# Second layer's routed experts computed on tokens sorted by expert, in 54 blocks of 128 laid among the attention's half steps, with the routing of all batches at once

## The chip, the cores and the metric

One core of one Trainium2 chip runs the whole program. The core has a matrix engine (TensorE; PE in the profile, its weight loads PEld), a vector engine (VectorE, DVE), an engine for functions and copies (ScalarE, ACT), a general engine (GpSimd, POOL) and an engine that here only issues transfers (SyncE, SP). Each engine works through its own program in order; engines wait for one another by semaphores, and data between DRAM and the on-chip memories moves by DMA, issued from a queue on one of the engines. Matrix products land in PSUM, a small memory of eight banks of 2 KB per partition; the rest of the on-chip data is in SBUF, 128 partitions wide.

The metric is the time of one execution in microseconds (us) on the device. All times below are in us unless marked ns.

## The reference, cut to what matters

The input is 2048 tokens (4 batches of 512) of 256 numbers, all in float32. There are two layers, each adding an attention and a mixture of experts, both of the normalised input, to the stream:

```python
xn = layernorm(x)
x = x + attention_0(xn) + experts_0(xn)   # 1 head of 256; 16 experts of width 176, 4 per token, and a shared one of width 352
xn = layernorm(x)
x = x + attention_1(xn) + experts_1(xn)

# attention_1: 8 groups of 4 query heads, head size 8, 512 keys per batch
sim = einsum('bgrsd,bgtd->bgrst', q, k) / sqrt(8)
out = softmax(sim) @ v                     # then a 256x256 projection

# experts_1: 7 routed experts and a shared one, all 256 -> 256 -> 256
def ffn(x, w1, wg, w2): return silu(x @ w1) * (x @ wg) @ w2
output = ffn(x, Ws1, Wsg, Ws2)
p = softmax(x @ gate_w + gate_b)
_, top = top_k(p + biases, 3)
w = p[top] / sum(p[top])                   # a weight for each of the 3 chosen experts
for e in range(7):
    output += ffn(x, W1[e], Wg[e], W2[e]) * (weight of e for this token, 0 if not chosen)
```

The softmax of the second attention has 32 heads x 512 x 512 scores per batch, with a contraction of only 8 numbers.

## The kernel before

**Layer 0.** After the attention of layer 0 the tokens are routed for all batches (`route`), sorted by expert into 79 slots of 128 rows, and each slot runs through `turn`, `gate_up`, `turn_back` and `down` (L576 to L640): rows are gathered from DRAM by an indirect DMA on POOL (L578), turned by TensorE (L586), multiplied by the weights of the slot's expert, which a register picks, and the result is copied (L637) and written to a DRAM table `y_rows` by a DMA on SP (L638). Later `combined` gathers each token's four rows from that table (L959, on POOL) and adds them with their shares on DVE (L978).

**Before the main loop** (L1076 to L1123). Batch 0 of layer 0 is combined, normalised and turned, its queries and keys are made (`project`), its experts are chosen (`choose`), and the pieces of the first layer's shared expert for all batches (`shared_pieces`) are laid between. The maxima of the first two units of attention are taken here (L1105).

**The main loop** (L1137 to L1197). The second attention runs in 32 units, (batch, unit) with 8 units of 4 heads in a batch. A unit is 4 tiles of 128 keys, each done in two *half steps*. A half step issues, in program order:

- a chore (`chore`, see below);
- `score_max` (L740): two matmuls of 32x512 for the unit two ahead, into the two banks `pa`, of which there is one copy;
- `score` (L779): two matmuls for the unit at hand, into `pb` (two copies);
- `take_max` (L752): one DVE reduction of 128x1024 out of `pa`;
- `exponentials` (L794): two ScalarE instructions of 128x512 out of `pb`;
- on every second half step `values` (L802) of the tile before, four matmuls; after a unit's last tile also `context`: a ScalarE copy (L816) and eight DMAs on SP (L820, L826);
- one *piece* of the experts.

`shift` closes a unit: a DVE transpose and 16 small DMAs on SP (L765) that put the maxima into the queries. The last two units have no unit two ahead; they run as 8 double steps (L1167 to L1183) with two pieces each.

**The experts before** are dense: every token runs through all 7 routed experts and the shared one. `expert_pieces` (L897) yields for each batch and each of the 8 experts four times a pair of pieces: `hidden` (L863, two matmuls of 128x512) with `gated` on each second one (a ScalarE tanh L875 and two DVE instructions L876, L877), and `down` (L882, two matmuls of 128x256, and a DVE instruction L893 that multiplies by the token's weight and adds to the stream). So pieces of `hidden` and of `down` alternate, one to a half step: 256 pieces, in 256 half steps.

**Chores** (L1038), one per half step: for batch b+1, while batch b's attention runs, they do layer 0's `combined`, the moments, `normalised`, `project` with its 28 DMAs on SP, and `choose`, which finds the three experts of a token and their weights; then `project_out` of batch b-1. `quotients` (L828) inverts the sums of the exponentials and sends them through DRAM.

**What sets the order.** TensorE, DVE and ScalarE run in the order written by hand. The order of the DMAs on SP and of the work on POOL is made by a scheduler. A tile has a fixed number of copies (`bufs`); who writes a copy again waits for the last reader of its former content, a DMA's end included. In PSUM before: `pa` two banks, `pb` two, `po`, `ph`, `pg` and `py` one each.

Of the kernel before, what the change touches and what calls it, by code (L numbers as in the profile page):

```python
# [40 lines left out]
W1P = 12  # L41
# [4 lines left out]
def two_layer_kernel(  # L46
# [67 lines left out]
    def normalised(layer: int, b: int, pool, psum, bo, tag: str, bufs: int, store=None, room=None):  # L114


        mv = stats[layer][:, ts(b, NQ), :]
        rstd = pool.tile([P, NQ], F32, tag="rstd", name=f"rstd{layer}_{b}")
        nc.vector.tensor_scalar(rstd, mv[:, :, 1], EPS, None, ALU.add)
        nc.scalar.activation(rstd, rstd, AF.Sqrt)  # L120
        nc.vector.reciprocal(rstd, rstd)
        yield
        for t in range(NQ):
            xn = (room or pool.tile)([P, H], F32, tag="xg" if room else "xn", name=f"xn{layer}_{b}_{t}")
            nc.vector.tensor_scalar(
                xn, xs[b][:, t, :], mv[:, t, 0:1], rstd[:, t : t + 1], ALU.subtract, ALU.mult
            )
            if store is not None:
                nc.gpsimd.dma_start(out=store[ts(b * NQ + t, P), :], in_=xn)
            yield "PE"  # L130
            pt = psum.tile([P, HC, P], F32, tag=tag, name=f"ptn{layer}_{b}_{t}", bufs=bufs)
            for c in range(HC):
                nc.tensor.transpose(pt[:, c, :], xn[:, ts(c, P)], ident)
            nc.scalar.copy(xnT[b][:, :, ts(t, P)], pt)
            if t == NQ - 1:
                nc.gpsimd.tensor_tensor(
                    xs[b], xs[b], bo.unsqueeze(1).to_broadcast([P, NQ, H]), ALU.add
                )
            yield
# [16 lines left out]
    y_rows = dram.tile([NS0 * P, H], F32, tag="y_rows", name="y_rows")  # L156

# [3 lines left out]
    with tc.tile_pool(name="w0", bufs=1, side="right") as w0:  # L161
# [17 lines left out]
        wqkv1s = whole(const, wqkv1, "wqkv1s")  # L179
        wo1s = whole(const, wo1, "wo1s")  # L180
        gate1s = whole(const, gate1, "gate1s")
# [12 lines left out]
        with tc.tile_pool(name="rt", bufs=1) as rt, tc.tile_pool(name="a0", bufs=2) as a0, tc.tile_pool(  # L194
            name="a0p", bufs=2, space=PSUM
        ) as a0p, tc.manual_schedule(engines={ENG.PE, ENG.DVE, ENG.Activation}):
            def counting(n: int, step: int, at: int, name: str):

                t = rt.tile([P, n], F32, tag=name, name=name)
                nc.gpsimd.iota(  # L200
                    t,
                    pattern=[[step, n]],
                    base=at,
                    channel_multiplier=1 if name == "tok" else 0,
                    allow_small_or_imprecise_dtypes=True,
                )
                return t

# [5 lines left out]
            def room(shape, dtype, tag: str, name: str):  # L214
                return w0.tile(shape, dtype, tag=tag, name=name, bufs=8)

            moments(0, 0, a0)
            first = normalised(0, 0, a0, a0p, bo, "pt", 2, xn_rows, room)
            next(first), next(first)
# [29 lines left out]
            for b in range(B):  # L249
                if b > 0:  # L250
                    first = normalised(0, b, a0, a0p, bo, "pt", 2, xn_rows, room)
                for _ in first:
                    pass
                if b + 1 < B:
                    moments(0, b + 1, a0)
                values0(b)

            lane = counting(P, 1, 0, "lane")
            slot = counting(NS0, 1, 0, "slot")
            tok = counting(NT, P, 0, "tok")  # L260
            full = counting(NT, P, 0, "full")
            ones = rt.tile([P, P], F32, tag="ones", name="ones")
            nc.gpsimd.memset(ones, 1.0)
            before = rt.tile([P, P], F32, tag="before", name="before")
            nc.gpsimd.affine_select(
                out=before,
                in_=ones,
                compare_op=ALU.is_gt,
                fill=0.0,
                base=0,  # L270
                pattern=[[1, P]],
                channel_multiplier=-1,
            )

            def summed(src, n: int, inner: int, name: str):

                bufs = []
                for i in range(2):
                    t = rt.tile([P, (8 + n) * inner], F32, tag=f"sum{i}", name=f"{name}{i}")
                    nc.gpsimd.memset(t[:, 0 : 8 * inner], 0.0)  # L280
                    bufs.append(t)
                nc.vector.tensor_copy(bufs[0][:, 8 * inner :], src)
                for i, d in enumerate((1, 2, 4, 8)):
                    x, y = bufs[i % 2], bufs[1 - i % 2]
                    nc.vector.tensor_tensor(
                        y[:, 8 * inner :],
                        x[:, 8 * inner :],
                        x[:, (8 - d) * inner : (8 - d + n) * inner],
                        ALU.add,
                    )  # L290
                return bufs[0][:, 8 * inner :]

            def route():
# [9 lines left out]
                top = rt.tile([P, NT, 8], F32, tag="top", name="top0")  # L303
                for t in range(NT):
                    nc.vector.max(out=top[:, t, :], in_=pr[:, t, :])
                    if t % 8 == 7:
                        yield
                nc.vector.memset(top[:, :, K0:8], -1.0)
                rest = rt.tile([P, NT, WP], F32, tag="rest", name="rest0")
                for t in range(NT):  # L310
                    nc.vector.match_replace(
                        out=rest[:, t, :],
                        in_to_replace=top[:, t, :],
                        in_values=pr[:, t, :],
                        imm_value=-2.0,
                    )
                    if t % 8 == 7:
                        yield

                mask = rt.tile([P, NT, E0], F32, tag="mask", name="mask0")  # L320
                nc.vector.tensor_tensor(mask, pr[:, :, 0:E0], rest[:, :, 0:E0], ALU.not_equal)
# [7 lines left out]
                upto = summed(cnt[:, 0, :], NT, E0, "ut")  # L329
                yield  # L330
                total = rt.tile([P, E0], F32, tag="total", name="total")
                nc.vector.tensor_copy(total, upto[:, (NT - 1) * E0 : NT * E0])
                pos = rt.tile([P, NT, E0], F32, tag="pos", name="pos")
                pflat = pos.rearrange("p t e -> p (t e)")
                nc.vector.tensor_tensor(pflat, upto, cnt[:, 0, :], ALU.subtract)
                nc.vector.tensor_tensor(pflat, pflat, cnt[:, 1, :], ALU.add)

                yield

                more = rt.tile([P, E0, NT], F32, tag="more", name="more")  # L340
                nc.vector.tensor_tensor(
                    more,
                    total.unsqueeze(2).to_broadcast([P, E0, NT]),
                    full.unsqueeze(1).to_broadcast([P, E0, NT]),
                    ALU.is_gt,
                )
                need = rt.tile([P, E0], F32, tag="need", name="need")
                nc.vector.reduce_sum(out=need, in_=more, axis=AX.X)
                yield
                end = summed(need, E0, 1, "en")  # L350
                base = rt.tile([P, E0], F32, tag="base", name="base")
                nc.vector.tensor_tensor(base, end, need, ALU.subtract)
                nc.vector.tensor_scalar(base, base, float(P), None, ALU.mult)

                yield

                of = rt.tile([P, NS0], F32, tag="of", name="of")
                half = (NS0 + 1) // 2
                for at in (0, half):
                    n = min(half, NS0 - at)  # L360
                    past = rt.tile([P, half, E0], F32, tag="past", name=f"past{at}")
                    nc.vector.tensor_tensor(
                        past[:, 0:n, :],
                        slot[:, at : at + n].unsqueeze(2).to_broadcast([P, n, E0]),
                        end.unsqueeze(1).to_broadcast([P, n, E0]),
                        ALU.is_ge,
                    )
                    nc.vector.reduce_sum(out=of[:, at : at + n], in_=past[:, 0:n, :], axis=AX.X)
                    yield
                nc.vector.tensor_scalar(off, of, float(E0 - 1), float(W0P), ALU.min, ALU.mult)  # L370

                yield
                nc.vector.tensor_tensor(
# [10 lines left out]
                for t in ith:  # L384
                    nc.gpsimd.memset(t[:, :, 0:8], 0.0)
# [274 lines left out]
    with tc.tile_pool(  # L660
# [236 lines left out]
        def expert_pieces():  # L897
# [16 lines left out]
            for t in range(NQ):  # L914
                down(*last[:2], t, last[2])
# [366 lines left out]
```

## Time and profile before

| what | us |
|---|---|
| median of 9 executions | 1330.07 (1325.77 to 1334.39) |
| the profiled execution | 1333.38 |
| its span (first to last instruction) | 1331.4 |
| mean granted TensorE clock in it | 0.973 of full speed |
| layer 0: attention | 0 to 165 |
| layer 0: the 79 slots | 165 to 360 |
| before the main loop | 360 to 474.8 |
| main loop, half steps 0 to 28 | 474.8 to 565.2 |
| main loop, half steps 29 to 190 | 565.2 to 1114.8 |
| main loop, half steps 191 to 239 | 1114.8 to 1272.7 |
| 8 double steps and the end | 1272.7 to 1331.4 |

The stage borders are starts of instructions of `score_max` or of the last units' scores. The main loop is cut at half steps 29 and 191, where the changed program changes what it lays between.

How to read the profile: one execution is recorded by the hardware. A page gives the busy time of each engine, the busy share and the granted TensorE clock (in tenths of full speed) in 40 equal slices, the chain of work that ended last with the share of each engine and line, and groups of instructions of the same line: form, count, busy time and mean duration, and how long the engine was idle just before them and on whose account. A timeline lists instructions by start, a window sums the busy time of each engine in a stretch. SPq is a queue of DMA issues on SP. Matmuls are pipelined, so their durations overlap; differences of starts are the safer measure.

### The profile page before, as it was taken

The numbers are of one execution on the slowest core, as the hardware profiler recorded it, in microseconds if no ns is written. First come the engines' busy times: TensorE is split into PE (matmuls) and PEld (weight loads), VectorE is DVE, ScalarE is ACT, GpSimd is POOL, SyncE is SP. The second block draws the span as 40 slices with busy tenths as digits, with TensorE's granted clock in tenths as the row PEclk, the third lists the DMA queues.
The fourth block names the chain that finished last, engine by engine and source line by source line (L and its number), as shares of the span: only waits on it lengthen the run. The fifth ranks groups of instructions, "written<-read, shape, count | busy, mean of one in ns | idle before, by whom it ended". The sixth has DMA issues, their size and how long they took to land.

```text
span 1331.4 us, 17659 instructions
## 1 busy us (share of the span) xinstructions
PE 1264.3 (95%) x6068; PEld 598.4 (45%) x6068; DVE 723.0 (54%) x1390; ACT 460.9 (35%) x929; POOL 189.2 (14%) x205
## 2 busy tenths in 40 slices
PE   5889999999999899999999999998999999999995
PEld 4456677777655333333323334432333433333332
DVE  5476244444452676546656656566654655465531
ACT  3321322222212025443434443342543334344342
POOL 4100263333050130000012000013000000000000
PEclk9899999999999689999999999998999999999998
DMA  9300133333133010001011001011000100000000
GB/s 359 128 1 8 56 117 108 107 104 107 62 125 147 15 48 4 10 10 25 16 29 39 8 5 30 13 33 55 4 10 9 26 24 5 9 23 4 10 8 24
DMA packets 43159, 64.04 MB, mean 48 GB/s; under 512 B 18816, under 2 KB 33120, under 8 KB 42176
## 3 DMA queue, kind: packets, MB, share of 16 engines
q1 hardware_dynamic: 33808, 34.00, 8.7%
q0 software_dynamic: 8064, 22.42, 5.8%
q10 hardware_dynamic: 1200, 6.51, 1.3%
q8 instruction: 49, 0.80, 0.2%
q14 instruction: 38, 0.31, 0.1%
HBM read 42.31 MB, written 14.81 MB: 43 GB/s over the span
## 4 chain that ended last, share of the span: by engine, by line
PE 89%; DVE 4%; DMA 2%; SPq 1%; issue 1%; ACT 1%; POOL 1%; ACTq 0%; DVEq 0%; POOLq 0%
PE pa L740 18%; PE ph L863 18%; PE py L882 10%; PE po L802 9%; PE pg L604 7%; PE py L628 5%; PE ps L927 3%; PE po L502 2%; PE pqk L463 2%; PE sc L471 2%; PE pa L620 1%; PE px L586 1%; PE po L844 1%; PE pys L941 1%; PE pv L240 1%
## 5 line engine op out<-in xcount | busy, mean ns | idle before, releaser
L794 ACT ACTIVATE ex<-pb 128x512 f32<-128x512 f32 x496 | 269.3, 595 | 452.3 <-PE pb L779 452.3
L752 DVE TENSOR_REDUCE mx<-pa 128x2 f32<-128x1024 f32 x248 | 302.8, 1221 | 154.7 <-PE pb L779 146.1
L740 PE MATMUL pa<-k,q 32*128 32x512 f32 x960 | 272.2, 643 | 14.4 <-DVE mx L752 14.4
L779 PE MATMUL pb<-q,k 32*128 32x512 f32 x960 | 272.7, 643 | 0.0
L882 PE MATMUL py<-ew,a 128*128 128x256 f32 x512 | 146.6, 409 | 1.7 <-DVE x L893 1.7
L882 PEld LDWEIGHTS py<-ew,a 128*128 128x128 f32 x512 | 87.7, 191 | 115.9 <-issue 105.2
L802 PE MATMUL po<-ex,v 128*32 128x512 f32 x1024 | 137.9, 610 | 0.0
L740 PEld LDWEIGHTS pa<-k,q 32*128 32x128 f32 x960 | 72.2, 184 | 144.2 <-DVE mx L752 78.3
L863 PE MATMUL ph<-xnT,ewg 128*128 128x512 f32 x256 | 131.3, 637 | 0.0
L863 PE MATMUL ph<-xnT,ew 128*128 128x512 f32 x256 | 130.3, 632 | 0.0
L893 DVE SCALAR_TENSOR_TENSOR x<-py,wt,x 128x256 f32<-128x256 f32 x112 | 54.2, 484 | 99.4 <-PE py L882 99.4
L604 PE MATMUL pg<-we,xT 128*128 x316 | 106.5, 460 | 0.5 <-issue 0.5
L959 POOL DMA_INDIRECT yk<-y_rows,place x64 | 61.5, 961 | 258.0 <-ACT ex L794 144.7
L578 POOL DMA_INDIRECT xg<-xn_rows,idx x79 | 75.0, 949 | 163.5 <-PE px L586 90.2
L615 DVE TENSOR_TENSOR a<-sg,pg 128x176 f32<-128x176 f32 x79 | 26.7, 338 | 106.0 <-ACT sg L613 106.0
L628 PE MATMUL py<-we,aT 88*128 x316 | 81.2, 379 | 0.0
L863 PEld LDWEIGHTS ph<-xnT,ewg 128*128 128x128 f32 x256 | 45.1, 195 | 79.9 <-issue 79.8
L863 PEld LDWEIGHTS ph<-xnT,ew 128*128 128x128 f32 x256 | 44.5, 193 | 80.4 <-issue 80.3
L779 PEld LDWEIGHTS pb<-q,k 32*128 32x128 f32 x960 | 72.7, 184 | 0.0
L802 PEld LDWEIGHTS po<-ex,v 128*32 128x32 f32 x1024 | 20.4, 108 | 97.6 <-issue 96.7
L604 PEld LDWEIGHTS pg<-we,xT 128*128 128x128 f32 x316 | 53.9, 190 | 17.5 <-issue 0.7
L876 DVE SCALAR_TENSOR_TENSOR th<-th,ph 128x512 f32<-128x512 f32 x64 | 44.0, 688 | 25.8 <-ACT th L875 25.7
(176 smaller groups left out, 1255.8 us busy)
## 6 DMA issues: line engine op xcount, KB each, us to landing
y_rows<-y SPq DMA_DIRECT2D x79, 128.0 KB
we<-in_dram SPq DMA_DIRECT2D x4, 2432.0 KB
q<-mt SPq DMA_DIRECT2D x512, 0.5 KB
ew<-in_dram ACTq DMA_DIRECT2D x2, 2048.0 KB
x<-in_dram SPq DMA_DIRECT2D x4, 512.0 KB
xn_rows<-xn POOLq DMA_DIRECT2D x16, 128.0 KB, 9.3
ewg<-in_dram ACTq DMA_DIRECT2D x1, 2048.0 KB
q<-qc SPq DMA_DIRECT2D x64, 32.0 KB
```

The costliest lines, as they stand in the source:

```text
L578: nc.gpsimd.indirect_dma_start(out=xg, out_offset=None, in_=xn_rows[:, :], in_offset=bass.IndirectOffsetOnAxis(ap=idx[:, s : s + 1], axis=0),)
L604: nc.tensor.matmul(pg, xT[s][:, c, :], we[:, ds(regs[s] + c * 2 * F0, 2 * F0)], start=c == 0, stop=c == HC - 1,)
L628: nc.tensor.matmul(py, actT[s][0:F0H, j, :], we[0:F0H, ds(regs[s] + HC * 2 * F0 + j * H, H)], start=j == 0, stop=j == 1,)
L740: nc.tensor.matmul(pa[:, i, :], q[at : at + ST, u, ts(t, P)], k[at : at + ST, 0, u % 2, :], start=True, stop=True, tile_position=(at, 0),)
L752: nc.vector.reduce_max(out=m[:, 0:16].rearrange("p (s t) -> p s t", t=NQ)[:, s0 : s0 + 2, t], in_=pa, axis=AX.X,)
L779: nc.tensor.matmul(pb, k[at : at + ST, 1, u % 2, ts(kc, P)], q[at : at + ST, u, :], start=True, stop=True, tile_position=(at, 0),)
L794: nc.scalar.activation(ex, pb, AF.Exp, scale=1.0 / math.sqrt(D1))
L802: nc.tensor.matmul(po[ts(s, ST), :], v[:, kc, half * 4 + s, :], exs[s], start=kc == 0, stop=kc == NQ - 1, tile_position=(0, s * ST),)
L863: nc.tensor.matmul(ps, (ew1, ewg)[which][:, c, e, ts(f, P)], xnT[b][:, c, :], start=c == 0, stop=c == HC - 1,)
L882: nc.tensor.matmul(py, a[:, f, ts(t, P)], ew2[:, f, e, :], start=f == 0, stop=f == F1 // P - 1,)
L893: nc.vector.scalar_tensor_tensor(xt, py, ewt[b][:, t, e : e + 1], xt, ALU.mult, ALU.add)
L959: nc.gpsimd.indirect_dma_start(out=yk[:, i, :], out_offset=None, in_=y_rows[:, :], in_offset=bass.IndirectOffsetOnAxis(ap=place[:, b * NQ ...
```

## The change

The routed experts of the second layer are no longer computed for all tokens. Each token's three (token, expert) pairs are sorted by expert into 54 slots of 128 rows, every expert filled up to whole slots: (2048 x 3 + 7 x 127) / 128 rounded down. The dense form had 7 x 16 = 112 pairs of expert and block. In `slots1` a slot is three pieces, one to a half step: `gate_up` (two matmuls of 128x512 with weights at an offset held in a register, then `gated` on 128x256), `turn` (four transposes: this slot's activation and the next slot's rows, and one ScalarE copy of 128x512), and down (two matmuls, a DVE copy to `y`, of which there is one copy, and an SP DMA to the DRAM table `y1_rows`). Rows are gathered on POOL three slots ahead.

All batches must be normalised and chosen before the first slot. So layer 0's sums are joined for all batches before the main loop (`combine0`); batches 0 and 1 are normalised there and 2 and 3 in the first half steps (`before_second`), followed by `route1`, which finds choice, counts and positions for all batches on DVE and POOL, with 48 index matmuls. The shared expert stays dense (`shared1`): batch 0 before the loop, batch 1 in half steps 0 to 14, batches 2 and 3 after the slots, a piece in every third half step. By the changed program's order the slots lie in half steps 29 to 190. From half step 192, `combine1` gathers three rows per token (48 indirect DMAs of 128 rows: 4 batches x 4 tiles x 3) and adds them on DVE, two per half step, through a tile with three copies. The last sixteen half steps (the 8 double steps) hold no pieces. Chores run twice per half step in batches 0 and 3.

The PSUM banks `ph`, `pg` and `py` become three copies of one tile `f`. Values and gate logits come from one product (`values_gate`). The second layer's weights lie expert by expert and are loaded in three parts. `project_out` of the batch before starts 12 half steps into the next.

```diff
+NS1 = (NT * P * K1 + E1 * (P - 1)) // P
...
+        def slots1():
...
+            def turn(s: int, act):
+                pt = filler([P, 2 * HC, P], f"px1_{s}")
+                t = a1.tile([P, 2 * HC, P], F32, tag="turn", name=f"turn{s}", bufs=1)
...
+                if s + 3 < NS1:
+                    gather(s + 3)
+                for j in range(lo, hi):
+                    src = act if j < HC else rows[s + 1]
+                    nc.tensor.transpose(pt[:, j, :], src[:, ts(j % HC, P)], ident)
+                nc.scalar.copy(t[:, lo:hi, :], pt[:, lo:hi, :])
...
+            for s in range(NS1):
...
+                pg = filler([P, 2 * F1], f"pg1_{s}")
+                for c in range(HC):
+                    nc.tensor.matmul(
+                        pg,
+                        x[:, HC + c, :],
+                        ew[:, ds(regs[s] + c * 2 * F1, 2 * F1)],
...
+                act = a1.tile([P, F1], F32, tag="act", name=f"act{s}", bufs=1)
+                gated(f"s{s}", pg[:, 0:F1], pg[:, F1:], act)
+                yield
+                turn(s, act)
+                yield
+                py = filler([P, H], f"py1_{s}")
...
+                y = a1.tile([P, H], F32, tag="y", name=f"y1_{s}", bufs=1)
+                nc.vector.tensor_copy(y, py)
+                nc.sync.dma_start(out=y1_rows[ts(s, P), :], in_=y)
+                yield
...
+        def combine1():
+            todo = [(b, t, k) for b in (B - 1, *range(B - 1)) for t in range(NQ) for k in range(K1)]
...
+                held[j] = a1.tile([P, H], F32, tag="xn", name=f"yk1_{j}", bufs=3)
+                nc.gpsimd.indirect_dma_start(
+                    out=held[j],
...
+                nc.vector.scalar_tensor_tensor(
+                    xt, held.pop(j), share1[:, b * NQ + t, k : k + 1], xt, ALU.mult, ALU.add
+                )
...
+            def fillers():
+                early = shared1(1)
+                while not routed:
+                    next(early, None)
+                    yield
+                    if not routed:
+                        yield
+                yield from early
+                yield from slots1()
+                last.append(combine1())
+                for b in (2, 3):
+                    for _ in shared1(b):
+                        for _ in range(3):
+                            yield
...
             def chore():
...
-                if due != "PE" or done % 4 in (1, 2):
-                    due = next(todo, None)
+                for each in (todo, last):
+                    while each and next(each[0], each) is each:
+                        each.pop(0)
...
-                    todo = chores(b + 1) if b + 1 < B else iter([None] * 8)
-                    if b > 0:
-                        todo = chain(todo, project_out(b - 1, *held.pop(b - 1)))
+                    if b == 0:
+                        todo.append(before_second())
+                    else:
+                        if b + 1 < B:
+                            todo.append(heads(b + 1))
+                        todo.append(until(step + 12))
+                        todo.append(project_out(b - 1, held.pop(b - 1)))
...
-                            piece()
+                            next(pieces, None)
+                            if b in (0, B - 1):
+                                chore()
```

## The prediction, made before the changed kernel had run

> **What bounds the kernel now.** I read the page first, then windows over the stages, a timeline of two half steps, and the SP queue. From the page:
>
> ```profile
> PE 1264.3 (95%) x6068; PEld 598.4 (45%) x6068; DVE 723.0 (54%) x1390; ACT 460.9 (35%) x929; POOL 189.2 (14%) x205
> ...
> PE 89%; DVE 4%; DMA 2%; SPq 1%; issue 1%; ACT 1%; POOL 1%; ACTq 0%; DVEq 0%; POOLq 0%
> ...
> L752 DVE TENSOR_REDUCE mx<-pa 128x2 f32<-128x1024 f32 x248 | 302.8, 1221 | 154.7 <-PE pb L779 146.1
> L740 PE MATMUL pa<-k,q 32*128 32x512 f32 x960 | 272.2, 643 | 14.4 <-DVE mx L752 14.4
> ...
> L882 PE MATMUL py<-ew,a 128*128 128x256 f32 x512 | 146.6, 409 | 1.7 <-DVE x L893 1.7
> ...
> L863 PE MATMUL ph<-xnT,ewg 128*128 128x512 f32 x256 | 131.3, 637 | 0.0
> L863 PE MATMUL ph<-xnT,ew 128*128 128x512 f32 x256 | 130.3, 632 | 0.0
> ```
>
> TensorE is busy 95% and makes 89% of the chain; the two lines of the dense experts are 131.3 + 130.3 + 146.6 = 408 us of it. The windows of the five stages say the same of the main loop: 537.07 busy of 549.60.
>
> ```profile
> 474.80:565.20 90.40, 88.50 (x469) 31.72 (x468) 60.82 (x88) 40.62 (x75) 12.75 (x12) 0.99 0.09 23
> 565.20:1114.80 549.60, 537.07 (x2773) 201.39 (x2773) 329.80 (x504) 221.16 (x411) 41.53 (x38) 0.99 0.09 20
> 1114.80:1272.70 157.90, 154.95 (x798) 55.94 (x798) 91.14 (x112) 61.98 (x116) 3.15 (x2) 0.99 0.04 10
> ```
>
> (Columns: length; busy time of PE, PEld, DVE, ACT, POOL; granted clock.) Then two half steps in the timeline:
>
> ```profile
> 961.36 0.70 PE L740 MATMUL pa<-k,q 32*128 32x512 f32 x2
> ...
> 962.43 1.98 PE L863 MATMUL ph<-xnT,ewg 128*128 128x512 f32 x4
> ...
> 962.53 1.23 DVE L752 TENSOR_REDUCE mx<-pa 128x2 f32<-128x1024 f32 x1 [0.58 <-PE pb L779]
> ...
> 964.35 0.70 PE L740 MATMUL pa<-k,q 32*128 32x512 f32 x2
> ...
> 965.42 1.06 PE L802 MATMUL po<-ex,v 128*32 128x512 f32 x8
> ```
>
> Scores take 962.43 - 961.36 = 1.07, `hidden` 964.35 - 962.43 = 1.92; values and `down` 1.0 and 1.06. So half steps with values take 1.07 + 1.00 + 1.06 = 3.13, those without 1.07 + 1.92 = 2.99: 6.1 a pair. But the same rows hold a second bound: the maximum starts 1.17 after its scores (962.53 - 961.36), takes 1.23, and the next scores need its banks (`pa` has one copy). No half step is shorter than about 1.17 + 1.23 + 0.05 = 2.45, whatever TensorE has left. **A half step can lose at most 0.6 us of its 3.05.** All 240 could lose 0.6 x 240 = 144 us plus chores; TensorE's saved work is not the measure.
>
> **The change, part by part.** The dense pieces that go (7 of 8 experts) were 7/8 x 408 = 357 us of TensorE. 54 slots add by the same rows 1.91 (two matmuls of 512) + 0.75 (four transposes; L586's take 273 ns each and overlap) + 1.06 = 3.7 each, 200 us. The attention keeps its 256 half steps.
>
> *Half steps 29 to 190 (slots), 549.6 before.* Three pieces against alternating halves make a cycle of six. Gate_up costs 1.07 + 1.91 = 2.98 or, with values, 3.98; down 2.45 (the maximum's bound) or 3.13. Turn has little TensorE work (1.82 or 2.82) but needs the activation: after gate_up a tanh (half of L875's 605 ns plus latency, 0.4 to 0.6), and two DVE instructions of 128x256 (484 ns for that size) stand ahead of the next maximum, 2.98 + 0.6 + 0.97 + 1.23 + 0.05 = 5.8 for two half steps: 2.8 each. Sum 2.98 + 2.82 + 2.45 + 3.98 + 2.80 + 3.13 = 18.16, against 18.33 before: **nothing is won where the slots run**. 27 cycles: 490. Chores left here (three `project_out`, two `heads`, quotients): 14.
>
> Then the new wait. `y` has one copy: each y copy on DVE waits for the former y's DMA, and that goes through SP behind the unit's 16 + 8 DMAs:
>
> ```profile
> 680.52 10.03 SPq L765 DMA_DIRECT2D q<-mt  x16
> 690.65 0.57 SPq L820 DMA_DIRECT2D sums<-o  x1
> ...
> 695.12 0.64 SPq L826 DMA_DIRECT2D cr<-o  x1
> ```
>
> SP is held from the border (680.5) until 15.2 us later. A y written in a unit's first half step leaves at 15 and lands at about 17.2 (landing of 128 KB is not shown: the 16 KB `quot` takes 1.4, the 512 KB output 3.4; I take 2.2). The next copy is due at 11.4; it, and the maximum queued behind it on DVE, wait 5.8. TensorE can run one half step ahead, so scores come 3.2 late. In a unit's second half step it costs 0.6, in the third 0. Of the 20 units in this stretch six hit each case: 6 x 3.2 + 6 x 0.6 = 23; in the three units in which SP also issues the 28 DMAs of the next heads and is held 33 us after the border (read in the same queue at a batch's start), the stores cost 7, 9 and 11: 27. Together 50 (bounds: 0, if the store goes out before the shift, and 80, if landing takes 4). Stalls leave clock windows half empty:
>
> ```profile
> 456.40:459.80 3.40, 1.99 (x15) 1.02 (x8) 2.52 (x4) 0.10 (x1) 0.00 (x0) 0.89 0.01 1
> 459.80:463.20 3.40, 3.40 (x6) 1.01 (x4) 3.06 (x4) 0.00 (x0) 0.00 (x0) 0.50 0.01 1
> ```
>
> After a window with TensorE busy 1.99 of 3.40 the next ran at half clock; in that part of the trace a `hidden` piece takes 3.7 in place of 1.9. So a long stall costs one slow window more: some 6 x 1.7 = 10. Sum 490 + 14 + 50 + 10 = **564**.
>
> *Half steps 0 to 28 (routing), 90.4 before.* TensorE loses pieces (a shared one every second step) but DVE gets the routing between maxima. Layer 0's `route` prices it: a row instruction 685 ns for 512, here 16 of 384 at 0.54; position steps 418 ns for 256 columns, here 112, about 0.25, some 50 of them; 32 small max and replace instructions at the 153 ns of L509; 17 index sums at 0.2, each behind three matmuls on columns that POOL makes (48, 315 ns each on DVE in layer 0). Two index steps per half step give 1.23 + 2 x (0.54 + 0.2) = 2.7 and a TensorE round trip of 0.5 to 0.9. Mean 3.7, up to 4.7: 29 x 3.7 = **107** (bounds 29 x 2.7 = 78 and 29 x 4.7 = 136).
>
> *Half steps 191 to 239, 157.9 before.* One shared piece in three half steps, DVE adds twice 0.48 in 25 of them, gathers two ahead (961 ns each on POOL, 2.7 to landing). At full clock 49 x 2.55 + 14 for `project_out`, piece-laden half steps and quotients = 139. TensorE is busy (1.07 + 0.5 + 0.5) / 2.5, some 60 to 80%, in many windows near the 1.99 of 3.40 above. At half clock a half step with values takes 2 x (1.07 + 1.00) = 4.1, one without about 3.3 (scores 1.07 later, less what overlaps): 3.7, so 1.15 more. With half of them slow: 139 + 24 x 1.15 = 167; with a quarter, 153. I take **155**.
> The Trainium skill ("TensorE: Matmul & The Clock Gate", "HAM oscillation") names only gaps of TensorE over about 3.4 us; by it nothing here would throttle, and this stretch would be 139, the sum 16 less. The rows above show half clock after a 59% busy window, so I don't follow it.
>
> *Before the loop, 114.8 before.* In come the shared expert of batch 0, 4 x 1.91 + 4 x 1.06 = 12, 48 more joins (64 in all, 484 ns; 23 us of DVE, idle there 64 of 115) and batch 1's normalisation; `choose` (5) and three pieces go. Gathers stay on POOL: 48 x 0.96 = 46 beyond its 27, inside the stretch. +13: **128** (bounds 115 and 141).
>
> *End, 58.7 before.* The double steps lose their pieces. One without pieces took 1307.66 - 1305.29 = 2.37, one with them 4.84. Gained 8 x 2.45 = 20; given back in part since the combination's last rows and half clock (the gaps of ScalarE-bound steps) remain: **48** (bounds 39 and 58). Layer 0 (360) stays.
>
> Sum: 360 + 128 + 107 + 564 + 155 + 48 + 2 outside the span = 1364, against 1333.4 for the profiled execution, which was 3.3 over the median. On the median's scale **1361**.
>
> **Rivals.**
> - *The y store doesn't wait* (faster). The stores leave SP before the shift or land early; nothing else changes. For it: all of SP's work per unit is 15 of 24 us, layer 0 issues the same store in 0.32 us. Against it: in the program's order these stores stand behind shift and context. Its price is the 50 + 10 above: 1301. It decides from 31 down: stalls below 60 - 28 = 32 us bring the time under 1333.
> - *The clock* (slower still). With all of 191 to 239 at half clock (181), routing and double steps too (each half step about 0.5 and 1.2 longer: 15 and 10): 1361 + 26 + 25 = 1412. For it: 0.50 stands in the windows above, and TensorE is no longer the bound. Against: 27 cycles of slots keep TensorE 93% busy.
> - *TensorE's saving counts in full*: 357 - 200 - 12 index and count matmuls = 145 less, 1185. Only the 2.45 bound speaks against it, and it stands in every half step.
>
> **How the numbers follow.** This kernel is measured to about 0.2%. Forecast (1335 to 1390) 0.50; store rival with part of the stalls, 1275 to 1333, 0.24; clock rival 1390 to 1425, 0.20; TensorE 0.01; the rest beyond 1425. The range 1285 to 1425 leaves out some 0.1 above and less below. Faster 0.24, within 0.2% 0.03, slower 0.73.
>
> **What would show it.** After: matmuls of the slots' lines some 200 us, TensorE's share near 83%; the y copy's idle time "until DMA y" some 50 us, in units' first half steps; half steps 29 to 190 at 562 to 566; half clock in the slices past the slots. Wrong if the y copies don't wait, if slot half steps fall under 3.0, or if routing exceeds 136.

## The result, and the profile after

The changed kernel took **1372.25 us** (median of 10, 1366.83 to 1375.44) against 1331.16 for the kernel before (31 executions): a ratio of **1.031, with a 95% interval of 1.0295 to 1.033**. The forecast was 1361. The profiled execution took 1375.75 us, its span 1374.0. By stretches, cut as before:

| stretch | before | forecast | changed | us at half clock, before / changed |
|---|---|---|---|---|
| layer 0 | 360 | 360 | 360 | 10 / 7 |
| before the main loop | 114.8 | 128 | 104.2 | 33 / 0 |
| half steps 0 to 28 (routing) | 90.4 | 107 | 132.3 | 1 / 41 |
| half steps 29 to 190 (slots) | 549.6 | 564 | 582.5 | 14 / 75 |
| half steps 191 to 239 | 157.9 | 155 | 150.4 | 3 / 24 |
| end | 58.7 | 48 | 44.6 | 10 / 14 |

(Us at half clock are summed from the granted clock that the trace records.) The page of the changed kernel, the lines that answer to those shown of before:

```profile
PE 1184.6 (86%) x5856; PEld 562.2 (41%) x5856; DVE 691.7 (50%) x1405; ACT 481.8 (35%) x979; POOL 318.4 (23%) x369
...
PE 66%; DVE 14%; SPq 8%; DMA 5%; issue 4%; ACT 2%; POOL 1%; DVEq 0%; ACTq 0%; POOLq 0%
...
L809 DVE TENSOR_REDUCE mx<-pa 128x2 f32<-128x1024 f32 x248 | 303.1, 1222 | 192.1 <-PE pb L836 176.4
L797 PE MATMUL pa<-k,q 32*128 32x512 f32 x960 | 292.2, 687 | 124.6 <-DVE mx L809 124.6
...
L1013 PE MATMUL pg<-ew,turn 128*128 x212 | 105.1, 618 | 0.0
L1035 DVE COPY y<-py 128x256 f32<-128x256 f32 x54 | 22.8, 422 | 122.7 <-DMA y_rows<-y 99.0
```

(L797 is the former L740, `score_max`; L809 the former L752, the maximum; L836 the former L779; L1013 the slots' first product; L1035 the copy to `y`.) TensorE's share of the chain fell from 89% to 66%, DVE's rose from 4% to 14%, and SP's queue and DMAs, 3% together before, now make 13%. Before, `score_max` waited 14.4 us for the maximum in all; now 124.6. The y copies were idle 99.0 us waiting for the former y's DMA. The main loop's three stretches, in windows (columns: length; busy time of PE, PEld, DVE, ACT, POOL; granted clock):

```profile
464.20:596.50 132.30, 102.34 (x543) 43.26 (x542) 75.08 (x209) 42.36 (x80) 43.89 (x58) 0.85 0.14 45
596.50:1179.00 582.50, 497.14 (x2647) 179.43 (x2646) 267.58 (x361) 241.31 (x459) 53.43 (x54) 0.94 0.13 33
1179.00:1329.50 150.50, 119.49 (x666) 36.69 (x665) 92.49 (x128) 58.62 (x108) 49.14 (x49) 0.92 0.21 60
```

TensorE is idle 30, 85 and 31 us in them (2, 13 and 3 before) and does part of its work at half clock. One store that is late, from the timeline of unit 20 (its first half step holds a slot's last product):

```profile
1071.95 10.07 SPq L822 DMA_DIRECT2D q<-mt  x16
...
1075.33 0.43 DVE L1035 COPY y<-py 128x256 f32<-128x256 f32 x1 [1.24 <-PE py L1027]
...
1086.61 0.64 SPq L883 DMA_DIRECT2D cr<-o  x1
1087.35 2.62 SPq L1036 DMA_DIRECT2D y_rows<-y  x2
...
1089.19 0.42 DVE L1035 COPY y<-py 128x256 f32<-128x256 f32 x1 [5.92 <-DMA y_rows<-y]
1089.53 1.22 DVE L809 TENSOR_REDUCE mx<-pa 128x2 f32<-128x1024 f32 x1
...
1090.80 0.70 PE L797 MATMUL pa<-k,q 32*128 32x512 f32 x2 [3.43 <-DVE mx L809]
```

The copy of 1075.33 is stored only at 1087.35, behind the sixteen DMAs of `shift` (L822) and the eight of `context` (L877, L883). The next copy waits until that store has landed, 1.8 us later; after it comes the maximum, and after that the scores, for which TensorE has stood idle for 3.43 us.

### The profile page after: what moved, and what is told of

It reads as the page before. It is cut to its first block, busy times and chain, and to the rows that moved or that the text cites. A ratio compares the mean times of both kernels' runs of the same rounds, so it can differ in the third digit from the quotient of the medians.

```text
span 1374.0 us, 18056 instructions
## 1 busy us (share of the span) xinstructions
PE 1184.6 (86%) x5856; PEld 562.2 (41%) x5856; DVE 691.7 (50%) x1405; ACT 481.8 (35%) x979; POOL 318.4 (23%) x369
## 4 chain that ended last, share of the span: by engine, by line
PE 66%; DVE 14%; SPq 8%; DMA 5%; issue 4%; ACT 2%; POOL 1%; DVEq 0%; ACTq 0%; POOLq 0%
PE pa L797 14%; PE po L859 8%; DVE mx L809 8%; PE pg L650 7%; PE pg L1013 5%; PE py L674 5%; PE ps L1081 3%; SPq L883 3%; SPq L877 2%; DMA y_rows<-y 2%; PE py L1027 2%; PE po L543 2%; PE pqk L504 2%; PE pb L836 2%; DMA yk<-y_rows,place 2%
## 5 line engine op out<-in xcount | busy, mean ns | idle before, releaser
L809 DVE TENSOR_REDUCE mx<-pa 128x2 f32<-128x1024 f32 x248 | 303.1, 1222 | 192.1 <-PE pb L836 176.4
L797 PE MATMUL pa<-k,q 32*128 32x512 f32 x960 | 292.2, 687 | 124.6 <-DVE mx L809 124.6
L836 PE MATMUL pb<-q,k 32*128 32x512 f32 x960 | 296.8, 686 | 0.0
L797 PEld LDWEIGHTS pa<-k,q 32*128 32x128 f32 x960 | 75.9, 193 | 251.3 <-DVE mx L809 205.6
L973 POOL DMA_INDIRECT xg<-xn_rows,idx x54 | 51.2, 949 | 461.0 <-PE px L989 459.9
L624 POOL DMA_INDIRECT xg<-xn_rows,idx x79 | 74.8, 946 | 163.4 <-PE px L632 90.4
L1013 PE MATMUL pg<-ew,turn 128*128 x212 | 105.1, 618 | 0.0
L1035 DVE COPY y<-py 128x256 f32<-128x256 f32 x54 | 22.8, 422 | 122.7 <-DMA y_rows<-y 99.0
L836 PEld LDWEIGHTS pb<-q,k 32*128 32x128 f32 x960 | 80.5, 193 | 0.0
L1116 POOL DMA_INDIRECT yk<-y_rows,place x64 | 61.5, 961 | 56.3 <-issue 44.0
L1049 POOL DMA_INDIRECT yk<-y_rows,place x48 | 46.8, 975 | 75.1 <-issue 56.6
L1013 PEld LDWEIGHTS pg<-ew,turn 128*128 128x128 f32 x212 | 35.9, 189 | 67.7 <-issue 67.7
L1027 PE MATMUL py<-ew,turn 128*128 x216 | 62.3, 412 | 0.0
L634 ACT COPY xT<-px 128x256 f32<-128x256 f32 x79 | 29.3, 372 | 82.4 <-PE px L632 77.6
L1027 PEld LDWEIGHTS py<-ew,turn 128*128 128x128 f32 x216 | 37.3, 193 | 49.6 <-ACT ex L851 25.9
## 6 DMA issues: line engine op xcount, KB each, us to landing
xn_rows<-xn POOLq DMA_DIRECT2D x16, 128.0 KB, 11.4
```

The source lines that it names most:

```text
L624: nc.gpsimd.indirect_dma_start(out=xg, out_offset=None, in_=xn_rows[:, :], in_offset=bass.IndirectOffsetOnAxis(ap=idx[:, s : s + 1], axis=0),)
L797: nc.tensor.matmul(pa[:, i, :], q[at : at + ST, u, ts(t, P)], k[at : at + ST, 0, u % 2, :], start=True, stop=True, tile_position=(at, 0),)
L809: nc.vector.reduce_max(out=m[:, 0:16].rearrange("p (s t) -> p s t", t=NQ)[:, s0 : s0 + 2, t], in_=pa, axis=AX.X,)
L836: nc.tensor.matmul(pb, k[at : at + ST, 1, u % 2, ts(kc, P)], q[at : at + ST, u, :], start=True, stop=True, tile_position=(at, 0),)
L973: nc.gpsimd.indirect_dma_start(out=rows[s], out_offset=None, in_=xn1_rows[:, :], in_offset=bass.IndirectOffsetOnAxis(ap=idx1[:, s : s + 1] ...
L1013: nc.tensor.matmul(pg, x[:, HC + c, :], ew[:, ds(regs[s] + c * 2 * F1, 2 * F1)], start=c == 0, stop=c == HC - 1,)
```

## The experiments

Four groups of runs were made, and the kernels of a group share runs of the kernel before: group 1 is the three copies of y, the first run of the store on POOL, the run without slots and the rows' store on POOL; group 2 the changed kernel again, the five row copies, the unread matmuls and both together; group 3 the second run of the store on POOL and the run with fewer of the matmuls; group 4 its third run and the five row copies again. In groups 1 and 3 the kernel before took 1343 and 1352 us in place of 1330 to 1333, and the stretch before the main loop took 128 to 142 us in every changed kernel, in place of 102 to 109: there ScalarE, DVE and TensorE stood still, once for 27.4 us, and the trace names no instruction or DMA that they waited for. Half steps 191 to 239 differ by group too: 156 to 161 us in groups 1 and 3 and 140 to 153 in the others, the run without slots set aside. So causes are read from half steps 29 to 190 above all, and other stretches and whole times are compared within a group.

**Three copies of y.**

```diff
-                y = a1.tile([P, H], F32, tag="y", name=f"y1_{s}", bufs=1)
+                y = a1.tile([P, H], F32, tag="y", name=f"y1_{s}", bufs=3)
...
-        EX = 10
+        EX = 9
...
-            sums0 = combine0(7)
+            sums0 = combine0(6)
```

> Three copies of the y tile instead of one (room for them: nine copies of the exponentials' tile instead of ten, and the sums of layer 0 gathered six ahead instead of seven). In the changed kernel the y copies on DVE were idle 99.0 us for the former y's DMA, in 17 waits. Theory A (the store's wait stalls DVE, the maxima behind it and so TensorE, and the half clock of this stretch follows from those stalls): that idle time falls under 5 us, half steps 29 to 190 fall from 582.5 to 495 to 515 us (27 cycles of 17.8 = 481, 14 of chores, some half clock), the half clock in them from 75 us to under 30, and the whole to 1285 to 1310. Theory B (the wait only moves: the rows, the gathers or SP are late as well, and the clock is half for want of work): the copies' idle time goes, but the stretch stays over 550 and the whole over 1340.

Half steps 29 to 190 took 504.8 us in place of 582.5, with 7 us of half clock in place of 75, and the copies' idle time for the former store fell from 99.0 us to 0.3. That is theory A. (A kernel of the same group that still stores y from one copy on SP, the run with the rows' store on POOL below, took 585.0 there, so it isn't the group.) The whole was 1335.49 against 1343.19 of before (ratio 0.9942, 0.9914 to 0.9969); the forecast 1285 to 1310 was missed, mostly by the stretch before the loop, 128.6 us here against 104.2.

**The store of y on POOL's queue.**

```diff
-                nc.sync.dma_start(out=y1_rows[ts(s, P), :], in_=y)
+                nc.gpsimd.dma_start(out=y1_rows[ts(s, P), :], in_=y)
```

> One copy of y as in the changed kernel, but its store is issued on POOL's queue instead of SP's. If the place behind the shift's and the context's DMAs on SP makes the wait (theory A), the store lands some 2 us after its issue, long before the next copy 9 us later: copies' idle time under 10 us, half steps 29 to 190 at 495 to 525, whole 1285 to 1320. If the landing itself is slow, or POOL's own program holds the store up (rival), the copies stay idle over 50 us and the whole stays over 1340.

Half steps 29 to 190: 503.9 us, with one copy of y as in the changed kernel. So it is not the landing that makes one copy too few, but the store's place on SP. The whole: 1330.39, ratio 0.9885 (0.9862 to 0.9908), above the expected 1285 to 1320, with 139 us before the loop. The same kernel was run twice more:

> The changed kernel with y's store on POOL's queue and nothing else, once more, since the first of these runs had a stretch before the loop of 139 us where later runs have 102 to 109. With that stretch at 102 to 109 the whole should be 1290 to 1305 (1375.6 of the changed kernel beside the later runs, less 79 in half steps 29 to 190): then the five copies and the deeper gathers of the other run gave less than 10 us. If it stays at 1320 or more, the deeper gathers were what helped.

> y's store on POOL's queue alone, beside the run with five row copies in the same group, since the stretch before the loop and half steps 191 to 239 came out longer in two of three groups, for the kernel before too. Half steps 29 to 190 at 500 to 505 as before in either case. If the shallow gathers are what makes half steps 191 to 239 long, they take 155 to 161 here whatever the group; if the group does, 141 to 150 in a quick one.

The first of them, in group 3, gave 1339.09 (ratio 0.9909, 0.9882 to 0.9937; before the loop 141.6; half steps 29 to 190: 501.5), over the 1320 that was to speak for the deeper gathers; the stretch before the loop was long again, so it couldn't decide that. The other gave **1295.38 us, ratio 0.9733 (0.9675 to 0.9791)**, with 104.7 before the loop and 501.6 in half steps 29 to 190. Its idle time ahead of the y copies, by what ended it, and its windows:

```profile
  PE py L1027: 24.9, 27
```

```profile
464.70:597.10 132.40, 102.53 (x541) 43.86 (x540) 74.97 (x209) 42.37 (x80) 43.92 (x58) 0.85 0.14 45
597.10:1098.70 501.60, 473.79 (x2647) 173.07 (x2646) 268.00 (x361) 240.98 (x459) 85.78 (x107) 1.00 0.15 38
1098.70:1251.70 153.00, 118.05 (x665) 36.55 (x664) 92.21 (x127) 58.54 (x108) 49.51 (x50) 0.92 0.20 59
```

No copy waits for a DMA any more, and the clock of the slots' stretch is 1.00. Set beside the changed kernel half step by half step, that kernel loses 80.9 us in this stretch. 61 of them lie in the 17 half steps in which a y copy waits for a late store; the other 20 are spread over the rest, some right behind a late store, and go with the half clock.

**The changed kernel once more**, for the comparison within a group:

> The changed kernel once more, unedited, on the chip of the runs beside it. In the first group of runs the kernel before took 1343 us, 12 more than elsewhere, and the stretch before the main loop took 129 to 139 us where the changed kernel's own trace has 104. If chips differ in that stretch, this run shows some 130 there and about 1385 to 1400 in all; if the edits made it longer, 104 and about 1372.

1375.63 us, ratio 1.033 (1.0298 to 1.0362), before the loop 109.2. The store on POOL, one and the same kernel, took 139.2, 141.6 and 104.7 us there in three groups. So the long stretch before the loop belonged to the group and not to the edits. What made it long wasn't found.

**No slots.** The routed experts are left out of the output; their half steps are empty.

```diff
-                yield from slots1()
-                last.append(combine1())
+                for _ in range(162):
+                    yield
+                for b in range(B - 1):
+                    leaves(b)
```

> Leaves out the 54 slots and the sum of their rows: the routed experts of the second layer are missing from the output; their half steps are empty, the rest (attention, shared expert, routing) stays. If a half step's floor is the maximum's round (1.17 + 1.23 + 0.05 = 2.45 us), half steps 29 to 190 take 162 x 2.46 = 399 + 14 of chores + 20 to 60 for half clock = 430 to 475 us, and the whole about 1225 to 1270. If TensorE's work counted in full, they would take 162 x 1.57 + 14 = 270 and the whole about 1060.

1265.74 us, one execution; half steps 29 to 190 took 462.0 us:

```profile
618.50:1080.50 462.00, 322.81 (x2005) 85.48 (x2004) 208.04 (x200) 192.14 (x351) 6.05 (x4) 0.91 0.08 15
```

```profile
703.56 1.23 DVE L809 TENSOR_REDUCE mx<-pa 128x2 f32<-128x1024 f32 x1 [2.77 <-PE pb L836]
...
704.84 0.70 PE L797 MATMUL pa<-k,q 32*128 32x512 f32 x2 [1.32 <-DVE mx L809]
...
706.01 1.23 DVE L809 TENSOR_REDUCE mx<-pa 128x2 f32<-128x1024 f32 x1 [1.23 <-PE pb L836]
...
707.29 0.70 PE L797 MATMUL pa<-k,q 32*128 32x512 f32 x2 [0.32 <-DVE mx L809]
```

Undisturbed half steps take 2.46 us, with or without values, though TensorE is busy only 323 of 462. That is the maximum's round: the scores of 704.84 and 707.29 each wait for the maximum before them. Had TensorE's work set the pace, the stretch was expected at 270. Taking away all work of the slots gains no more than 501.6 - 462.0 = 40 us over the kernel with the early store, in part because the clock falls in the empty half steps (0.91).

**The normalised rows' store on POOL's queue.**

```diff
-            centred(1, b, t, rstd, xn, nc.sync, xn1_rows)
+            centred(1, b, t, rstd, xn, nc.gpsimd, xn1_rows)
```

> As the changed kernel, but the normalised rows of the second layer are stored from POOL's queue instead of SP's, where eight of them took from 471.4 to 492 among the shift's DMAs. If the SP queue holds the routing stretch up (its xn tile has three copies that wait for their stores), half steps 0 to 28 fall from 132 us to 115 to 125. If the stretch is set by DVE's routing instructions, the moments ahead of it and half clock, they stay at 128 to 134 and the whole within 4 us of 1372.

Half steps 0 to 28: 133.3 us, as in the changed kernel. The rows' store on SP isn't what holds the routing up. The whole, expected within 4 us of 1372, was 1394 to 1418 (median 1412.69; ratio 1.0425, 1.0359 to 1.049); the profiled execution, 1416.61, has 134.3 us before the loop, 30 more than the changed kernel's profile, as others of group 1 do.

**Five row copies, and the sums gathered four ahead**, with the store on POOL (and, to make room, nine copies of the exponentials' tile and layer 0's sums gathered six ahead):

```diff
-                held[j] = a1.tile([P, H], F32, tag="xn", name=f"yk1_{j}", bufs=3)
+                held[j] = a1.tile([P, H], F32, tag="xn", name=f"yk1_{j}", bufs=5)
...
-            for j in range(2):
+            for j in range(4):
                 gather(j)
...
-                if j + 2 < len(todo):
-                    gather(j + 2)
+                if j + 4 < len(todo):
+                    gather(j + 4)
```

> As the run with y's store on POOL's queue, and the row tile has five copies instead of three, with the second layer's sums gathered four ahead instead of two (nine copies of the exponentials' tile). If the waits of those sums for their gathers lengthen half steps 191 to 239 (157.8 us, steps of 4 to 6 us in units 24 to 26), they fall to 135 to 145. If the half clock or the other work on DVE sets them, they stay over 152.

> The run with five row copies again. If the deeper gathers shorten half steps 191 to 239, they take at least 8 us less here than in the run beside it; if it was the group, the two differ by less than 5 us in every stretch and by less than 10 us in all.

The first run gave 1295.63 (ratio 0.9734, 0.9708 to 0.976) and 141.6 us in half steps 191 to 239, against 145.2 of the changed kernel in the same group. Beside the store alone in one group, the second gave 145.3 there against 153.0, but 137.8 against 132.4 in half steps 0 to 28 (half clock 55 against 41), and the whole was the same: 1296.38 against 1295.38. So the deeper gathers shorten their own stretch by some 8 us, just short of what was expected, and the whole not by anything that can be told.

**Matmuls that nobody reads**, with the store on POOL, to hold the clock:

```diff
+            def warm(n: int):
+                for i in range(n):
+                    nc.tensor.matmul(
+                        filler([P, S], f"warm{step}_{i}"),
+                        xnT[0][:, 0, 0:P],
+                        xnT[0][:, 0, :],
+                        start=True,
+                        stop=True,
+                    )
...
-                    next(early, None)
+                    if next(early, early) is early:
+                        warm(1)
                     yield
                     if not routed:
+                        warm(2)
                         yield
...
                     for _ in shared1(b):
-                        for _ in range(3):
+                        yield
+                        for _ in range(2):
+                            if step % 2:
+                                warm(1)
                             yield
```

> As the run with y's store on POOL's queue, with matmuls of 128x512 that nobody reads in half steps without a piece: one or two in half steps 0 to 28, one in those without values from 191 on, 0.95 us each at full clock. If the half clock lengthens these stretches, 0 to 28 fall from 131 us to 112 to 122 and 191 to 239 from 158 to 140 to 150, with half clock under 10 us in each. If DVE and the gathers set them, they stay within 4 us or grow by the added work, whatever the clock.

> Both edits together on top of the store on POOL. If the gathers and the clock are separate causes, the gains add: 1290 to 1310 where the run with the store alone took 1330. If they are one cause (the clock is half because TensorE waits for the sums), the two together give no more than the better one, within 4 us.

```profile
462.40:587.00 124.60, 114.94 (x607) 49.72 (x606) 75.28 (x209) 42.38 (x80) 44.07 (x58) 0.99 0.15 49
587.00:1088.70 501.70, 473.89 (x2647) 173.19 (x2646) 267.85 (x361) 240.84 (x459) 85.76 (x107) 1.00 0.15 39
1088.70:1230.80 142.10, 124.78 (x697) 39.53 (x696) 91.86 (x127) 58.58 (x108) 49.15 (x50) 1.00 0.22 64
```

The whole took **1282.59, ratio 0.9634 (0.9603 to 0.9666)**, 93 us under the changed kernel in the same group, the lowest of all here. The two edits together gave 1284.46 (0.9648, 0.9621 to 0.9676): 11 us under the deeper gathers without the matmuls, and no better than the matmuls alone. So it is the added work that shortens the whole, and the deeper gathers add nothing to it that can be told.

The stretches show less. Half steps 191 to 239 run at full clock with the matmuls, but are little shorter for it: 142.1 us with the matmuls, 141.6 with the deeper gathers, 139.8 with both, 145.2 for the changed kernel, all in one group. In half steps 0 to 28 the matmuls left 124.6 us (3 us of half clock; 112 to 122 were expected) and, with the deeper gathers, 128.6 (10 us); kernels with slots but without the matmuls took 128.7 to 137.8 (31 to 55 us) over all groups.

Fewer of the matmuls, with the store on POOL:

> As the run with unread matmuls, but in the routing stretch only one of them in each second half step, and none from half step 18 on, where the index matmuls run and TensorE was busy 30.00 of 30 us with them. If the added matmuls stood in the way there, half steps 0 to 28 fall from 124.6 to 114 to 121 us and the whole to 1272 to 1280; if without them the clock falls to half again, the stretch stays at 124 to 130 us with over 10 us of half clock.

The clock fell again (31 us of half clock) and half steps 0 to 28 took 128.5: the second alternative. But the same kernel without any of them took 128.7 in this group, with as much half clock, so the few that were left did nothing there. Half steps 191 to 239, where all of them stayed, took 156.8 against 161.4. The whole, 1332.79 (ratio 0.9869, 0.9809 to 0.9928), isn't clear of the 1339.09 beside it.

## Why the prediction was right, and where it wasn't

The direction and its main cause were forecast and hold, and the size roughly: 31 us slower was forecast and 41 measured. But that the sum came out so close, 1361 against 1372, is partly luck: two terms of it, routing and the stretch before the loop, were off by some 24 us each, in opposite directions, and what is left is mostly a third, the slots' stretch, 18 us too low.

- **The bound of a half step** (2.45 us by the maximum) holds: 2.46 in the run without slots and in the slots' shortest half steps. That run's 462 us, where TensorE's work alone would have made 270, excludes the rival that the saving counts in full.
- **"Nothing is won where the slots run."** The undisturbed cycle measures 2.65 + 2.46 + 3.98 + 2.59 + 3.13 + 2.99 = 17.80 us against the 18.16 forecast; turn was priced 0.2 too long. Times 27 that is 481, and with the store out of the way the stretch takes 501.6, 21 for chores and the first slots in place of 14.
- **The wait for the y store** was the right mechanism, and undersized: 81 us with its half clock, not 60. The two terms were 50 and 10; the half steps with a waiting copy cost 61, the rest 20. A store in a unit's first half step made the next copy idle 4.3 to 6.3 (5.8 forecast) and cost 1.9 to 3.9, 3.0 in the mean of seven (3.2). In the second half step it cost 2.6 in four of six units, not 0.6: the 15.2 us that SP is held were counted from the unit's border, but in the changed kernel the transpose ahead of `shift` can stand behind a slot's two gating instructions on DVE. At unit 12, whose border is at 837.85, the timeline of DVE has

```profile
838.38 0.42 DVE L932 SCALAR_TENSOR_TENSOR ths<-ths,pg 128x256 f32<-128x256 f32 x1 [1.08 <-ACT ths L931]
838.83 0.42 DVE L933 SCALAR_TENSOR_TENSOR act<-ths,pg 128x256 f32<-128x256 f32 x1
839.17 0.20 DVE L818 STREAM_TRANSPOSE mt<-mx 128x32 f32<-128x32 f32 x1
```

  so the shift's DMAs started at 839.44, and the y store left at 854.82, 17.0 after the border. The stores behind the heads' DMAs cost 11 and 16 where 9 and 11 were forecast, and 2 where 7 was. Two of the signs named beforehand were off with it: the copies' idle time was 99.0 us and not some 50, and 75 us of half clock lay among the slots, where it was looked for past them.
- **Routing** failed: 132.3, not 107, though inside its bounds. The step "Mean 3.7" priced every half step as a maximum, two index steps and a round trip to TensorE. The trace shows what was left out: in the first half step (7.8 us) the moments of two batches, eight times 0.40 + 0.18 us, stand ahead of the first maximum, beside two loads of a function table for ScalarE of 1.28 each; and the last (11.4 us) waits for the first slot's rows and then runs the next heads' products, partly at half clock:

```profile
591.21 0.69 PE L989 MATMUL px_-1_5058<-ident,xg 128*128 128x128 f32 x2 [3.99 <-DMA xg<-xn_rows,idx]
591.48 0.55 PEld L749 LDWEIGHTS pq<-xnT,wqk1s 128*128 128x128 f32 x2
591.69 4.85 PE L749 MATMUL pq<-xnT,wqk1s 128*128 128x512 f32 x8
```

  Half clock (41 us there, none forecast in this stretch) is probably part of it: with the unread matmuls and 3 us of half clock the stretch is 124.6, 8 less, but with 10 us of it in the other such run 128.6, no less than the 128.7 that the store on POOL took once without them. Even at 124.6, 17 over the forecast remain. The first and last half steps, 7.8 and 8.1 us there, are some 8 of them; the rest no run took apart. (The 153 ns taken for max and replace instructions is the time of a reciprocal; theirs are 156 to 166 ns, with 84 more for a load of values in each replace. That makes under 2 us.)
- **Before the loop** failed the other way: 104.2, not 128. The step added the new work to 114.8. But 33 of those 114.8 us ran at half clock, and with pieces and joins laid between there was none: TensorE was busy 99.87 us in place of 105.93, with more matmuls. That the full clock is a reason is read from the two traces and was not tried by itself; 33 us at half clock can account for at most some 16 us of the 24, so the rest of the miss stays open. The stretch also fell below its lower bound of 115.
- **Half steps 191 to 239 and the end** came within 5 us in the profile of the changed kernel (150.4 and 44.6); its second profile has 145.2 for the half steps. I had taken a quarter of the windows as slow; 24 and 10 us of some 150 were. Relieving the gathers gained 4 and 8 us here (145.2 to 141.6 and 153.0 to 145.3, each within a group), holding the clock 3 and 5 (145.2 to 142.1 and 161.4 to 156.8).
- **The rival that the y store doesn't wait** was worked out at 1301, and the store moved to POOL gave 1295. That the two are close is luck again: the price of the wait, 60, was some 20 too low, and the forecast that it was taken from 11 too low. But the wait alone decided the sign, as forecast: 81 us gone is more than the 41 lost.
- **The clock rival** (1412) did not come as it was described: half clock was longest in the slots' stretch (75 us), where it went when the store's wait went, and half steps 191 to 239 had 24 us of it and not all.

The Trainium skill's rule ("TensorE: Matmul & The Clock Gate", "HAM oscillation") names gaps over about 3.4 us. In the changed kernel's trace the clock fell as well after nine windows of 3.4 us that were busy for 43 to 61% with no gap in TensorE's work longer than 2.1 us. The measurement decides: half clock did come in half steps 191 to 239, and they took 150.4 and 145.2 us, so part of the 16 us that the rule would have taken off was due, though not all.

## What to carry to other kernels

Before pricing work taken off the busiest engine, find the next bound of the loop's step: here a maximum on DVE between two products let no half step fall below 2.45 us, and some 157 us less of TensorE's work (357 - 200, the forecast's estimate) could win little. A tile with one copy ties its writer to the whole queue on which its store stands: look at what that queue is doing at that moment, or give the store another queue; moving one line here turned 3.1% slower into 2.7% faster. And where a stretch leaves TensorE partly idle, allow for half clock in part of it (24 of 150 us in half steps 191 to 239 here, 82 of 462 in the run without slots); some products that nobody reads took 11 us off the whole in one comparison, and an unclear 6 in another with fewer of them.

## What the runs showed of the hardware that was not expected

- Adding work to TensorE shortened the whole: 1284.46 against 1295.63 us in one group, the same kernel with and without the unread matmuls.
- A store of 128 KB from SBUF landed some 1.8 us after its issue, but on SP it was issued 12 us after the copy that it stores where a unit's 24 DMAs stood ahead of it, and up to 24 us after it where the next heads' DMAs did too.
- The same kernel's stretch before the main loop, rich in indirect gathers, took 104.7 us in one group and 141.6 in another, and three engines waited there for nothing that the trace shows. The cause is open.
